# A transformer block on one core: sums moved ahead of the last additions at the MLP's change of layers, and one square root moved into the next QKV

## The chip, the cores and the metric

The kernel runs on one core of one Trainium2 chip. The metric is the device time of one execution in microseconds, as the median of several runs. Beside the runs there is one profiled execution, whose trace is read here. The core has TensorE (PE; its weight loads are listed as PEld), VectorE (DVE), ScalarE (ACT), GpSimd (POOL) and SyncE (SP), which issues most of the transfers. Each engine executes its own queue in order, and semaphores hold an instruction until its inputs and its output's room are ready.

## What is computed

A transformer block with adaptive layer norm on two sequences (rows 0 and 1) of 2048 tokens with 512 features, 16 heads of 32, all in float32:

```python
mod = silu(condition) @ Wada + bada
sh_a, sc_a, gt_a, sh_m, sc_m, gt_m = split(mod, 6)
xm = layernorm(x, g1, be1) * (1 + sc_a) + sh_a
x = x + gt_a * attention(xm, Wqkv, Wproj, bproj)     # causal, softmax
xm = layernorm(x, g2, be2) * (1 + sc_m) + sh_m
h = gelu(xm @ W1 + b1)                               # 512 -> 2048
x = x + gt_m * (h @ W2 + b2)                         # 2048 -> 512
```

## The kernel before

The stages stand one after the other: QKV of row 0, attention of row 0, projection of row 0, QKV, attention and projection of row 1, and then the MLP over both rows. Large products are made by Strassen's scheme in Winograd's form: seven products, named A11, S1, S2, S4, S3, A12, A22 in the order in which `seven` and `two_level` issue them, in place of eight. Their operands are sums and differences of blocks, made by VectorE or GpSimd. The products accumulate in PSUM banks and are combined from there by VectorE (`combine`, line 1728) or copied by ACT.

Most instructions go through `act` or `mm`, which keep them in the order in which the program issues them on their engine. What is queued behind a waiting instruction waits too.

**Projection of a row** (`project_phase`). For each of 16 token tiles: TensorE makes the product, VectorE adds it to the residual (line 1348) and takes the tile's statistics (lines 219 and 222) for the MLP's layer norm, kept in `mv2`. After the last tile `inv_std` turns the 16 variances of the row into `rstd2` and `shift2`: a square root on ACT (line 225), a reciprocal and a product on VectorE (lines 226, 227). They are read only when the MLP normalizes that row's tokens. Right behind the projection of row 0 comes the QKV of row 1: `Qkv.run` issues steps, one outer product each, and after each step calls `tick`, which calls `also(g, n)` with the group g of 512 tokens and the step's number n, from 0. `first` in it (line 1060) lets ACT copy a product's bank, so that the bank can go on.

**The MLP** goes over four groups m of 1024 tokens. For each group the first layer makes the hidden units pair by pair: `pair_of_sets` (m = 1, 2, 3; four pairs p = 0 to 3) makes two units of each half of the 2048 for all tokens, with `two_level` in three phases. Each half of the units (first index) and each half of the tokens (second) gives one of d00, d01, d10, d11, two tiles of 128x512 each. After phase 2 four additions of the third term `t3` finish d11 and d10 (`add`, line 2221), and four gelus (`gelu`, line 2214) follow. In the pairs p = 0 to 2 the additions run on GpSimd and the gelus are put into the next pair's first phase (`later[0]`). In the last pair (`final`) the additions run on VectorE and the gelus follow at once on ACT.

Then `tail` makes the second layer: seven outer sets A11, S1, A12, S2, S3, A22, S4, each of the seven products again (`outer`, one call of `seven`). Each product takes eight matmuls of 256 columns. The operands of the inner products are differences of parts of h (`difference`, line 1631; 128x1024). `Hidden.todo` lists them in the order of use, as keys such as (A11, 2), the second sum of outer set A11. `pop` issues the next one; `need` issues all up to those that a product is about to read. In the last pair's phases four of them are issued through `among`, all to GpSimd: (A11, 1), two parts of T1, (S1, 1). In `tail`, `then(k)` is called after product k of a set and pops one more, to VectorE. The third product (S2) of outer set A11 reads (A11, 2), the fifth (S3) reads (A11, 3), the seventh (A22) reads (A11, 4).

The sums stand in a list of shared tiles (`sums`), PSUM has four banks with the tag "mm" for `outer`, of which each set takes three, and for the transposes of the next group's tokens, which take two after the sets of m < 3.

Of the kernel before, what the change touches and what calls it, by code (L numbers as in the profile page):

```python
# [27 lines left out]
def dit_block_kernel(  # L28
# [192 lines left out]
            act(ins)  # L221
        nc.vector.bn_aggr(mv[:, n, :], st)

    def inv_std(mv, rstd, shift, lo, hi):
        nc.scalar.activation(rstd[:, lo:hi], mv[:, lo:hi, 1], AF.Sqrt, bias=eps)
        nc.vector.reciprocal(rstd[:, lo:hi], rstd[:, lo:hi])
        nc.vector.scalar_tensor_tensor(
            shift[:, lo:hi], mv[:, lo:hi, 0], -1.0, rstd[:, lo:hi], ALU.mult, ALU.mult
        )

    def rows_of(psum, r, b, tag):
# [1066 lines left out]
    def project_phase(row, psum, between):  # L1298

        b = row.b
        with pool(f"proj{b}") as pp:
            n = 0
            ats = list(row.at_s)
            rbs = {1: row.rb_s[1], 2: row.old_queries(), 3: row.rb_s[0]}
            rows_x = [b * NT + i * TQ + t for i in last_order for t in range(TQ)]
            xts = list(row.xt_s)

            def tokens(upto):
                while len(xts) < min(upto, NT):
                    xt = pp.tile([P, D], F32, tag="xt", name="xt", bufs=6)
                    nc.sync.dma_start(xt, x_rows(rows_x[len(xts)]))
                    xts.append(xt)

            row.load_sums(len(units) - 1, len(units))
            tokens(TQ + 6)
            for k, i in enumerate(last_order):
                if k in (0, 1):  # L1320

                    at = pp.tile([P, C, QB], F32, tag="at", name="at", bufs=2)
                    nc.sync.dma_start(at, od[b][last_order[k + 2]])
                    ats.append(at)
                at = ats[k]
                for t in range(TQ):

                    if n == 0:
                        nc.sync.dma_start(rbs[2], wide_d[b][last_order[2]])
                        nc.sync.dma_start(  # L1330
                            rbs[3][:, : C - 1], wide_d[b][last_order[3]][:, : C - 1]
                        )
                    elif n == 3:
                        row.invert(len(units) - 1, len(units))
                    elif n == 4:
                        row.widen(len(units) - 1, rbs[3][:, C - 1, :])

                    tokens(n + 6)
                    nt, xt = rows_x[n], xts[n]
                    if k > 0:  # L1340
                        act(nc.gpsimd.tensor_tensor(xt, xt, bgate, ALU.add))
                    ps = psum.tile([P, D], F32, tag="mm", name="ps_o")
                    for c in range(C):
                        mm(
                            ps, at[:, c, t * P : (t + 1) * P], row.wproj[:, c, :],
                            start=(c == 0), stop=(c == C - 1),
                        )
                    nc.vector.tensor_tensor(xt, ps, xt, ALU.add)
                    stats(pp, xt, nt, mv2, True)
                    nc.sync.dma_start(x1d[nt], xt)  # L1350
                    if k + 1 < NQ:
                        d = ats[k + 1][:, t, :]
                        act(
                            nc.gpsimd.tensor_tensor(d, d, rbs[k + 1][:, t, :], ALU.mult)
                        )
                    between(n)
                    n += 1
        lo, hi = b * NT, (b + 1) * NT
        inv_std(mv2, rstd2, shift2, lo, hi)


    row = Row(0)
# [167 lines left out]
    with pool("qkv1") as qp, pool("ps_qkv1", bufs=6, space=PSUM) as ps_mm:  # L1530
        qkv = Qkv(row, qp, ps_mm)
        qkv.xts[0] = past.next_s

        def between(n):
            if n == 6:
                qkv.load_w(nc.gpsimd)
            if 9 <= n < 12:
                qkv.weight_sum(nc.vector, n - 9)
            elif n == 13:
                qkv.weight_sum(nc.gpsimd, 3)  # L1540
            if n >= 12:
                qkv.token_sum(0, (S1, S2, S3, A22)[n - 12])

            if n < MTT:
                qkv.stats(0, n, True)
            if n in (5, 8):
                qkv.norm(0, n // 8)()
            if n == 8:
                qkv.load_x(1)
            if n >= NT - MTT:  # L1550
                qkv.stats(1, n - (NT - MTT), True)

        project_phase(past, ps_mm, between)

        def also(g, n):
            if (g, n) == (0, 10):
                qkv.value_weight_sums()
            pieces.tick()

        with pool("hl1") as hp:  # L1560
            qkv.load_wv(hp, nc.gpsimd)
            pieces = Pieces()
            spare_q = [row.old_queries().rearrange("p h q -> p (h q)") for _ in range(2)]
            spare_k = [row.key_room(q) for q in (2, 3)]

            def room_1():
                return [
                    (0, blocks_of(value_rows(row, 4, 8), w2p)),
                    (2, blocks_of(value_rows(row, 8, NT), w2p)),
                    (6, blocks_of(spare_q[0], w2p)[:, 1:]),  # L1570
                ]

            def room_3():
                return [
                    (0, blocks_of(value_rows(row, 8, NT), w2p)),
                    (4, blocks_of(spare_k[1], w2p)),
                    (6, blocks_of(spare_q[0], w2p)[:, 1:]),
                ]

            for f, (room, load, start) in enumerate((  # L1580
                (room_2, 0, 6), (room_1, 16, 24), (room_2, 47, 56), (room_3, 74, 80),
            ), FC // 2):
                pieces.plan(f, room, load, start)
            qkv.run(hp, also)
            pieces.done()
# [8 lines left out]
    with ExitStack() as mlp:  # L1594
# [246 lines left out]
        class Hidden:  # L1841
# [3 lines left out]
            def __init__(self):  # L1845
# [6 lines left out]
                ]  # L1852
                self.todo, self.made, self.at = [], set(), 0
                self.slots, self.later, self.flip = {}, {}, False
                self.t = {n: {} for n in OUTER}
                x = {
                    (g, half): {
# [340 lines left out]
            def pair_of_sets(self, p, among):  # L2198
# [13 lines left out]
                def gelu(half, d, j):  # L2212
                    act(
                        nc.scalar.activation(
                            d[j], d[j], AF.Gelu, bias=col(r_b1 + half * HF + fs[j], 1)
                        )
                    )

                def add(engine, d, x):
                    for j in range(2):  # L2220
                        act(engine.tensor_tensor(d[j], d[j], x[j], ALU.add))  # L2221

                def phase(ph, jobs):
# [38 lines left out]
                    4: [lambda: gelu(0, d01, 0)], 6: [lambda: gelu(0, d01, 1)],  # L2262
                }
                phase(2, ((A22, d10, d10), (S3, t3)))
                add(nc.vector if final else nc.gpsimd, d11, t3)
                add(nc.vector if final else nc.gpsimd, d10, t3)
                ends = [
                    lambda d=d, j=j: gelu(1, d, j) for d in (d11, d10) for j in range(2)
                ]
                if final:  # L2270
                    for f in ends:
                        f()
                else:
                    self.later[0] = {r: [f] for r, f in enumerate(ends, 3)}

# [69 lines left out]
        def tail(m, hid, among, each):  # L2345

            u, c22, c11, c12 = Y
            later = []

            def gate(y, half):
                later.extend(lambda i=i: gated(m, y, half, i) for i in range(2))

            for n, dst, base in (
                (A11, u, None),  # L2360
                (S1, c22, None),
                (A12, c11, u),
                (S2, u, u),
                (S3, u, u),
                (A22, u, u),
                (S4, c12, c12),
            ):

                def then(k):
                    if k in (1, 3) and later:  # L2370
                        later.pop(0)()
                    hid.pop()
                    among(n, k)

                hid.outer(n, dst, base, then, each if n == S4 else None)
                if n == A12:
                    gate(c11, 0)
                elif n == S2:
                    combine(c12, u, c22)
                elif n == S3:  # L2380
                    combine(c22, c22, u)
                    gate(c22, 1)
                elif n == A22:
                    gate(u, 1)
                elif n == S4 and not each:
                    gate(c12, 0)
            for f in later:
                f()
# [137 lines left out]
```

## Time and profile before

| | us |
|---|---|
| median of three runs | 2253.81 |
| lowest, highest | 2253.27, 2258.36 |
| profiled execution, its time | 2258.55 |
| profiled execution, its span | 2256.8 |
| mean granted clock of TensorE | 0.995 |

The span goes from the first to the last instruction. A row of waits has the waiting engine, tile and line, what released it, and then total time, number of times and the longest. A row of the timeline has start and duration in us, engine, line, operation, output and inputs, shape and count of merged instructions; in brackets the engine's idle time before it and what ended that. A row of windows has the stretch, its length, the busy time of PE, PEld, DVE, ACT and POOL, the granted clock (1.00 is full), the DMA engines' busy share and GB/s. A row of one line's instructions has their count, duration in ns (min/median/max), first and last start, and shapes. Line numbers are those of the kernel before.

### The profile page before, as it was taken

The page shows a single profiled execution, that of the slowest core. Times are in us where ns is not written, and L with a number is a line of the kernel's source. Part 1 is how long each engine was busy: PE and PEld are TensorE (multiplying, and loading weights), DVE is VectorE, ACT ScalarE, POOL GpSimd, SP SyncE. Part 2 cuts the span into 40 slices and gives each one's busy share as a digit, 9 for nine tenths or more (in the row PEclk, how much of TensorE's full clock was granted, in tenths as well). Part 3 has the DMA queues.
Part 4 walks back from the last instruction along what each step waited for, and adds up shares of the span by engine and source line. Part 5 has one row for each costly group of instructions (what it writes and reads, how often), then busy time and mean ns, then how long its engine had stood idle before and what let it go on. Part 6 is the DMA issues. An engine that isn't in the chain of part 4 may idle for free.

```text
span 2256.8 us, 34324 instructions
## 1 busy us (share of the span) xinstructions
PE 2202.7 (98%) x12273; PEld 1475.6 (65%) x12273; DVE 1577.0 (70%) x3385; ACT 1038.1 (46%) x2132; POOL 1429.7 (63%) x891
## 2 busy tenths in 40 slices
PE   7999999999999999999999999999999999999998
PEld 5887555555543588755555555345788888888887
DVE  4678767777757667777677766664686686677576
ACT  4434555655564243355656556513324423532510
POOL 4253998998983695299989898448417516605520
PEclk9999999999999999999999999999999999999999
DMA  8787142231324799533324123367656455554543
GB/s 271 247 277 192 43 93 70 62 85 48 107 95 147 241 308 312 157 77 74 73 75 95 48 60 133 107 228 262 212 167 213 146 178 180 189 163 159 191 149 108
DMA packets 166627, 340.99 MB, mean 151 GB/s; under 512 B 17216, under 2 KB 49516, under 8 KB 164664
## 3 DMA queue, kind: packets, MB, share of 16 engines
q1 hardware_dynamic: 158080, 302.05, 44.0%
q0 software_dynamic: 8000, 36.21, 4.3%
q8 instruction: 97, 1.59, 0.3%
q14 instruction: 74, 0.61, 0.1%
q10 hardware_dynamic: 376, 0.55, 0.1%
HBM read 246.46 MB, written 100.14 MB: 154 GB/s over the span
## 4 chain that ended last, share of the span: by engine, by line
PE 87%; DVE 6%; POOL 3%; DMA 2%; ACT 1%; issue 1%; SPq 0%; DVEq 0%; ACTq 0%; POOLq 0%
PE ps_a L207 23%; PE st L207 18%; PE ps_b L207 13%; PE o L207 10%; PE s L207 9%; PE ps_c L207 4%; PE sm L207 3%; PE ps_o L207 2%; DVE junk L499 1%; POOL ee L696 1%; PE ps_xt L215 1%; ACT e L671 1%; DVE mx L505 1%; DVE h L2221 1%; PE ps_o L215 1%
## 5 line engine op out<-in xcount | busy, mean ns | idle before, releaser
L671 ACT ACTIVATE e<-st 128x512 f32<-128x512 f32 (+1 forms) x1152 | 574.8, 578 | 362.4 <-PE st L207 313.6
L505 DVE TENSOR_REDUCE mx<-s 128x1 f32<-128x512 f32 x576 | 381.8, 686 | 193.8 <-PE s L207 192.8
L696 POOL TENSOR_TENSOR ee<-ee,e 128x2048 f32<-128x2048 f32 x106 | 485.9, 4584 | 10.3 <-ACT e L671 4.4
L207 PE MATMUL st<-qst,kst 128*128 128x512 f32 (+3 forms) x1280 | 408.6, 386 | 0.0
L207 PE MATMUL s<-kst,qst 128*128 128x512 f32 (+3 forms) x1046 | 380.6, 395 | 5.7 <-DVE mx L505 3.7
L207 PE MATMUL ps_a<-sum,w 128*128 128x256 f32 (+1 forms) x1304 | 340.9, 396 | 12.3 <-DVE sum L1631 11.7
L207 PE MATMUL o<-e,vv 128*32 128x512 f32 (+3 forms) x2560 | 293.2, 537 | 0.3 <-POOL e L683 0.3
L207 PEld LDWEIGHTS st<-qst,kst 128*128 128x128 f32 x1280 | 228.5, 188 | 97.7 <-issue 65.9
L207 PEld LDWEIGHTS ps_a<-sum,w 128*128 128x128 f32 x1304 | 249.2, 193 | 55.3 <-ACT c L2317 12.8
L499 DVE CUSTOM_DVE_ANT_0 junk<-s,causal 128x128 bf16<-128x128 f32 (+3 forms) x470 | 220.7, 470 | 61.0 <-PE s L207 47.0
L207 PEld LDWEIGHTS s<-kst,qst 128*128 128x128 f32 x1046 | 194.8, 188 | 70.7 <-DVE mx L505 17.0
L696 POOL TENSOR_TENSOR ee<-e 128x2048 f32<-128x2048 f32 x42 | 192.5, 4584 | 42.6 <-ACT e L671 42.6
L207 PE MATMUL ps_b<-sum,w 128*128 128x256 f32 (+1 forms) x744 | 186.5, 381 | 0.0
L2221 POOL TENSOR_TENSOR h<-h,h 128x512 f32<-128x512 f32 x96 | 119.3, 1273 | 69.6 <-DVE h L1728 69.6
L207 PEld LDWEIGHTS <-sel 32*128 32x128 bf16 x1152 | 29.5, 91 | 197.0 <-issue 196.1
L207 PEld LDWEIGHTS ps_b<-sum,w 128*128 128x128 f32 x744 | 140.7, 190 | 21.7 <-issue 2.6
L1793 POOL TENSOR_TENSOR sum<-xm 128x256 f32<-128x256 f32 x22 | 23.1, 1052 | 185.4 <-PE ps_a L207 185.4
L505 DVE TENSOR_REDUCE mx<-st 128x1 f32<-128x512 f32 x192 | 131.1, 683 | 0.5
L683 POOL TENSOR_SCALAR_AFFINE_SELECT e<-e 128x512 f32<-128x512 f32 x128 | 83.3, 669 | 67.4 <-ACT e L671 67.3
L207 PEld LDWEIGHTS o<-e,vv 128*32 128x32 f32 x2560 | 59.1, 108 | 92.4 <-issue 73.3
L207 PE MATMUL st<-fold,sel 32*128 32x512 bf16 (+1 forms) x1152 | 117.5, 372 | 1.3
L1067 POOL TENSOR_TENSOR lo<-lo,hi 128x512 fp32r<-128x512 f32 x32 | 40.6, 1275 | 104.4 <-ACT hi L1065 99.4
(264 smaller groups left out, 3549.9 us busy)
## 6 DMA issues: line engine op xcount, KB each, us to landing
w<-w1x SPq DMA_DIRECT2D x42, 896.0 KB
qst<-q SPq DMA_DIRECT2D x128, 256.0 KB
kst<-k SPq DMA_DIRECT2D x128, 256.0 KB
w<-w2d SPq DMA_DIRECT2D x28, 1024.0 KB
w<-w2d SPq DMA_DIRECT2D x28, 768.0 KB
q<-hi SPq DMA_DIRECT2D x32, 256.0 KB
q<-lo SPq DMA_DIRECT2D x32, 256.0 KB
k<-hi SPq DMA_DIRECT2D x32, 256.0 KB
```

What stands on the lines that cost most here:

```text
L207: return tc.keep_in_program_order(nc.tensor.matmul(*args, **kw))
L215: return tc.keep_in_program_order(nc.tensor.transpose(dst, src, ident[:n, :n]))
L499: nc.vector.tensor_tensor_reduce(junk[:, :w], x, causal[:, QB - w :], 1.0, MASKED, ALU.add, ALU.max, m,)
L505: self.vector(nc.vector.tensor_reduce(m, x, axis=AX.X, op=ALU.max))
L671: act(nc.scalar.activation(e4[:, h, :w], sts[h][:, :w], AF.Exp))
L683: nc.gpsimd.affine_select(d, d, pattern=[[0, HC], [1, P]], compare_op=ALU.is_ge, fill=0.0, base=0, channel_multiplier=-1,)
L696: act(nc.gpsimd.tensor_tensor(dst, x, y, ALU.add))
L1067: engine.tensor_tensor(lo, d, hi.bitcast(F32), ALU.subtract)
L1793: act(engine.tensor_tensor(dst, u, v, ALU.subtract))
L2221: act(engine.tensor_tensor(d[j], d[j], x[j], ALU.add))
```

## The change

Row 0's `inv_std` leaves the end of the projection and is issued in the QKV of row 1, in group 0 after step n = 8, with its three instructions kept in program order. Row 1's stays.

In `pair_of_sets` the last additions run on GpSimd in every pair, d10 ahead of d11, and the gelus follow in this order too. In the last pair the sums (A11, 2) to (A11, 4) are issued ahead of the additions, and the four gelus are handed to `tail`, which issues one each after products k = 4, 5, 6 of outer set A11 and after the first product of S1. There `then` pops no sum after products 0 and 1 of A11, so that from k = 2 on each sum has the place it had. At m = 0, which uses `pair`, nothing changes.

```diff
-    def inv_std(mv, rstd, shift, lo, hi):
-        nc.scalar.activation(rstd[:, lo:hi], mv[:, lo:hi, 1], AF.Sqrt, bias=eps)
-        nc.vector.reciprocal(rstd[:, lo:hi], rstd[:, lo:hi])
-        nc.vector.scalar_tensor_tensor(
-            shift[:, lo:hi], mv[:, lo:hi, 0], -1.0, rstd[:, lo:hi], ALU.mult, ALU.mult
+    def inv_std(mv, rstd, shift, lo, hi, keep=False):
+        order = act if keep else (lambda ins: ins)
+        order(nc.scalar.activation(rstd[:, lo:hi], mv[:, lo:hi, 1], AF.Sqrt, bias=eps))
+        order(nc.vector.reciprocal(rstd[:, lo:hi], rstd[:, lo:hi]))
+        order(
+            nc.vector.scalar_tensor_tensor(
+                shift[:, lo:hi], mv[:, lo:hi, 0], -1.0, rstd[:, lo:hi],
+                ALU.mult, ALU.mult,
+            )
         )
...
-        lo, hi = b * NT, (b + 1) * NT
-        inv_std(mv2, rstd2, shift2, lo, hi)
+        if b:
+            inv_std(mv2, rstd2, shift2, NT, 2 * NT)
...
             if (g, n) == (0, 10):
                 qkv.value_weight_sums()
+            elif (g, n) == (0, 8):
+                inv_std(mv2, rstd2, shift2, 0, NT, True)
...
+                self.ends = []
...
                 phase(2, ((A22, d10, d10), (S3, t3)))
-                add(nc.vector if final else nc.gpsimd, d11, t3)
-                add(nc.vector if final else nc.gpsimd, d10, t3)
+                if final:
+                    self.need(*[(A11, n) for n in (2, 3, 4)])
+                add(nc.gpsimd, d10, t3)
+                add(nc.gpsimd, d11, t3)
                 ends = [
-                    lambda d=d, j=j: gelu(1, d, j) for d in (d11, d10) for j in range(2)
+                    lambda d=d, j=j: gelu(1, d, j) for d in (d10, d11) for j in range(2)
                 ]
                 if final:
-                    for f in ends:
-                        f()
+                    self.ends = ends
                 else:
                     self.later[0] = {r: [f] for r, f in enumerate(ends, 3)}
...
                 def then(k):
                     if k in (1, 3) and later:
                         later.pop(0)()
-                    hid.pop()
+                    if hid.ends and (n != A11 or k >= 4):
+                        hid.ends.pop(0)()
+                    if n != A11 or k > 1 or not hid.ends:
+                        hid.pop()
                     among(n, k)
```

## The prediction

> **What bounds the kernel now.** I read the page from the top, then the waits of TensorE alone, then three stretches of the timeline and of the windows. The page:
>
> ```profile
> span 2256.8 us, 34324 instructions
> PE 2202.7 (98%) x12273; PEld 1475.6 (65%) x12273; DVE 1577.0 (70%) x3385; ACT 1038.1 (46%) x2132; POOL 1429.7 (63%) x891
> ...
> PE 87%; DVE 6%; POOL 3%; DMA 2%; ACT 1%; issue 1%; SPq 0%; DVEq 0%; ACTq 0%; POOLq 0%
> ```
>
> TensorE is busy for 98% of the span and holds 87% of the chain that ended last, so only what TensorE waits for, or what slows it, has a price. The waits of TensorE, columns total, times, longest:
>
> ```profile
> PE ps_a L207 <- DVE sum L1631: 11.7, 3, 3.9
> ...
> PE ps_a L207 <- ACT lo L1060: 2.9, 2, 2.7
> ```
>
> The first is the longest total of all of TensorE's waits; its three times are the three changes of layer of the MLP (m = 1, 2, 3). The second holds one wait of 2.7 us, after the first row's projection. The two edits sit on just these places.
>
> **The change of layers.** The timeline at m = 3 (start, duration, engine, line):
>
> ```profile
> 2149.57 0.73 ACT L2214 ACTIVATE h<-h,cols 128x512 f32<-128x512 f32 x1
> ...
> 2150.42 4.70 POOL L1631 TENSOR_TENSOR sum<-h,h 128x1024 f32<-128x1024 f32 x2
> ...
> 2153.17 0.42 DVE L1728 TENSOR_TENSOR h<-h,ps_a 128x256 f32<-128x256 f32 x1
> ...
> 2153.40 1.89 PE L207 MATMUL ps_a<-h,w 128*128 128x256 f32 x8
> 2153.51 6.11 DVE L2221 TENSOR_TENSOR h<-h,y 128x512 f32<-128x512 f32 x4
> ...
> 2155.13 1.89 PE L207 MATMUL ps_b<-sum,w 128*128 128x256 f32 x8
> 2155.20 2.68 POOL L1631 TENSOR_TENSOR sum<-sum,sum 128x1024 f32<-128x1024 f32 x1
> 2155.70 0.72 ACT L2214 ACTIVATE h<-h,cols 128x512 f32<-128x512 f32 x1 [1.10 <-DVE h L2221]
> 2158.46 1.95 ACT L2214 ACTIVATE h<-h,cols 128x512 f32<-128x512 f32 x3 [2.03 <-DVE h L2221]
> 2159.55 1.21 DVE L1631 TENSOR_TENSOR sum<-h,sum 128x1024 f32<-128x1024 f32 x1
> ...
> 2160.68 1.21 DVE L1631 TENSOR_TENSOR sum<-h,h 128x1024 f32<-128x1024 f32 x1
> ...
> 2160.91 3.75 PE L207 MATMUL ps_a<-sum,w 128*128 128x256 f32 x8 [3.89 <-DVE sum L1631]
> ...
> 2167.47 1.89 PE L207 MATMUL ps_a<-sum,w 128*128 128x256 f32 x8
> ```
>
> The outer products of A11 start at 2153.40, one each 1.73 us (2153.40 to 2155.13). The third, S2, needs sum (A11, 2), which is queued on VectorE behind the four last additions (6.11 us): it starts at 2159.55 and TensorE idles 3.89 us. Then TensorE is slow as well: eight matmuls take 3.75 us in place of 1.89, in a window whose granted clock (the column of 0.50) is half:
>
> ```profile
> 2163.00:2164.00 1.00, 1.00 (x3) 0.76 (x3) 1.00 (x2) 0.00 (x0) 0.00 (x0) 0.50 0.00 0
> ```
>
> So the price is read over four products, from S1's start to S3's, which should lie 3 x 1.73 = 5.19 us apart. Here they are 2167.47 - 2155.13 = 12.34 apart: 7.15 lost. The same rows at m = 1 and 2:
>
> ```profile
> 1789.27 1.89 PE L207 MATMUL ps_b<-sum,w 128*128 128x256 f32 x8
> ...
> 1795.04 3.62 PE L207 MATMUL ps_a<-sum,w 128*128 128x256 f32 x8 [3.88 <-DVE sum L1631]
> ...
> 1800.23 1.89 PE L207 MATMUL ps_a<-sum,w 128*128 128x256 f32 x8
> ...
> 1971.74 1.89 PE L207 MATMUL ps_b<-sum,w 128*128 128x256 f32 x8
> ...
> 1977.53 3.75 PE L207 MATMUL ps_a<-sum,w 128*128 128x256 f32 x8 [3.90 <-DVE sum L1631]
> ...
> 1983.62 1.89 PE L207 MATMUL ps_a<-sum,w 128*128 128x256 f32 x8
> ```
>
> 10.96 - 5.19 = 5.77 and 11.88 - 5.19 = 6.69. **Together 19.61 us**, of which 11.67 are the three idle times and 7.94 the slow clock behind them.
>
> *What goes away.* `need` puts sums (A11, 2) to (A11, 4) ahead of the additions. They read d00 after its gelus (ended by 2149.57 + 0.73 = 2150.30) and tiles long free, so (A11, 2) can issue where the first addition does now, at 2153.51.
>
> *What they meet there.* GpSimd has two sums queued that end at 2150.42 + 4.70 = 2155.12. An addition takes VectorE 0.68 us alone and up to 2.83 beside GpSimd; GpSimd takes 1.27:
>
> ```profile
> L2221 POOL TENSOR_TENSOR h<-h,h x96: 1252/1272/1295, 1710.4 to 2149.2; 128x512 f32<-128x512 f32 x96
> ...
> L2221 DVE TENSOR_TENSOR h<-h,y x12: 678/1417/2832, 1787.6 to 2158.9; 128x512 f32<-128x512 f32 x12
> ```
>
> The first addition was issued at 2153.51 and its gelu waited to 2155.70: it ended some 0.55 after GpSimd's sum (2155.12). The next ended near 2158.4, 0.55 after GpSimd's next sum (2155.20 + 2.68 = 2157.88). So the two take turns, one instruction each. VectorE's additions out of PSUM keep 0.42 (2153.17, inside GpSimd's sum), so they take no part. The Trainium skill, "SBUF — State Buffer", section "Who interferes with whom", says that a VectorE instruction with two SBUF inputs and a GpSimd one that reads SBUF lock each other out whole, by issue order; these rows agree.
>
> I play the turns forward (a sum ends 1.21 - 0.13 = 1.08 after its grant, a GpSimd addition 1.10): (A11, 2) ends 2156.2, GpSimd's (S1, 1) 2158.4, (A11, 3) 2159.5, d10's first addition 2160.6, (A11, 4) 2161.7, d10's second 2162.8, a T1 sum 2163.8, d11's first 2164.9, the other T1 sum 2166.0, d11's second 2167.1, (S1, 2) 2168.2. Then GpSimd has nothing left. TensorE, unstalled, asks for (A11, 2) at 2156.86, (A11, 3) at 2160.3, (A11, 4) at 2163.8, and in the next set for (S1, 2) at 2165.5 + 3.45 = 2168.9. **Each is there in time**, by 0.7, 0.8, 2.1 and 0.7 us.
>
> *What is late next.* The combination of the A12 product, behind (S1, 2), ends at 2168.5 in place of 2165.9. It frees one of four PSUM banks; the second product of the next set takes that bank at m = 1 and 2, where the transposes of the next tokens come between (at m = 3 it takes another):
>
> ```profile
> 1805.41 1.04 PE L215 MATMUL ps_xt<-ident,xn 128*128 128x128 f32 x8
> ```
>
> That product is due at 2165.5 + 0.87 + 1.73 = 2168.1 on m = 3's clock, and the bank comes 0.6 us later, with the 0.15 that a release takes (S2 started at 2160.91, its sum ended at 2159.55 + 1.21 = 2160.76). I charge 0.6 twice, **1.2 us**; bounds 0 (the turns go a little faster) and 3 x 2.2 = 6.6 (first rival). VectorE has caught up a set later: in S1 it has seven sums at 1.13 (2159.55 to 2160.68) and three combinations at 0.42, 9.2 us, within 7 x 1.73 = 12.1 us of TensorE.
>
> *The four gelus.* At 0.73 each they go from the end of the pair to the last three steps of A11 (k = 4, 5, 6) and the first of S1. ACT reaches them at 2162.0, 2163.8, 2165.9 and 2168; their inputs are there at 2160.6, 2162.8, 2164.9, 2167.1. Queued behind them are ACT's copies that free banks; none is held, so 0. First reader of the result is (A12, 2), after the last. Without that cover a late addition delays TensorE us for us (slow rival). The swap of d10 and d11 in the other pairs changes which of two equal additions goes first, nothing else: 0.
>
> **The variances of row 0.** The end of its projection:
>
> ```profile
> 771.53 1.03 PE L207 MATMUL ps_a<-xmT,wqk 128*128 128x256 f32 x4
> ...
> 772.40 1.03 PE L207 MATMUL ps_b<-t,wqk 128*128 128x256 f32 x4
> ...
> 773.84 0.69 DVE L1348 TENSOR_TENSOR xt<-ps_o,xt 128x512 f32<-128x512 f32 x1 [3.11 <-POOL xt L1341]
> ...
> 775.30 0.18 DVE L222 BATCH_NORM_AGGREGATE mv<-stat 128x2 f32<-128x6 f32 x1
> 775.52 0.31 ACT L225 ACTIVATE rstd<-mv,eps 128x16 f32<-128x16 f32 x1 [8.35 <-DVE mv L222]
> 775.73 0.36 ACT L1060 ACTIVATE lo<-ps_a 128x256 f32<-128x256 f32 x1
> ...
> 775.86 0.25 DVE L226 RECIPROCAL rstd<-rstd 128x16 f32<-128x16 f32 x1 [0.37 <-ACT rstd L225]
> ...
> 776.14 0.18 DVE L227 SCALAR_TENSOR_TENSOR shift<-mv,rstd 128x16 f32<-128x16 f32 x1
> ...
> 776.15 1.13 PE L207 MATMUL ps_a<-t,wqk 128*128 128x256 f32 x4 [2.73 <-ACT lo L1060]
> ```
>
> ACT stands at the square root until the last token tile's statistics (775.48), with the copies of ps_a and ps_b (products of 771.53 and 772.40) behind it; TensorE needs the first copy and idles **2.73 us**. Moved to the ninth step of the next QKV, the root leaves ACT free: the copies can run as each product ends. VectorE is in the late tile to 775.48, while its first combination is due two products after ps_b's, about 775.1; the six banks of this stage absorb that. At the new place three small instructions cost 0.31 on ACT and 0.25 + 0.18 + 0.37 wait on VectorE, between products 0.87 apart: 0, hidden behind TensorE's next products (the whole 0.7 if VectorE's combination were the next thing asked for). A reload of ACT's table is not to be expected, since the roots here stand among copies as before; the rows of line 225 have three for ten roots, and one more would hold ACT for 1.28, inside what the banks absorb:
>
> ```profile
> L225 ACT ACT_TABLE_LOAD  x3: 1283/1283/1283, 28.4 to 1514.4; - x3
> ```
>
> I take a gain of 2.73; bounds 0 (it is waited for later, below) and 2.73.
>
> **The sum**, against the profiled execution: 2258.55 (span 2256.8) - 19.61 + 1.2 - 2.73 = **2237.4**. That execution lies 4.7 above the median of 2253.81; one unprofiled run was as long (2258.36) and one 2253.27. The three clock dips above are of unequal cost at equal idle times (1.89, 2.79 and 3.26 at 3.9 us), so I read much of the spread as that: it would go with the dips, and all runs come to 2237. If it is something else, 2232.7 follows. I take **2236.5**, nearer the first. The Trainium skill, "TensorE: Matmul & The Clock Gate", section "What's actually happening", has the clock judged over free-running windows of about 3.4 us, so the same idle time would cost differently from run to run; the unequal dips fit that. No run here shows it yet.
>
> **Rivals.**
> *GpSimd first* (0.08): the turn at 2155.12 goes to (S1, 1), and (A11, 2) ends at 2157.88 + 1.08 = 2158.96: TensorE idles 2.2 us at each change, 6.6 in all, with a dip for each at up to 7.94 in all: 2243 to 2251. For it: GpSimd's next sum is issued 0.08 after the last. Against: VectorE got that turn in the rows above.
> *Row 0's gain is given back* (0.08): GpSimd's work of the next QKV starts with weight loads that do not move, and TensorE, 2.7 us ahead, waits for it: 2239. Against it, GpSimd runs dry before it is next on the path:
>
> ```profile
> 861.79 1.27 POOL L1067 TENSOR_TENSOR lo<-lo,hi 128x512 fp32r<-128x512 f32 x1 [10.78 <-ACT hi L1065]
> ```
>
> *The change does not do what it says* (0.04): something else holds (A11, 2), and only row 0 gains: 2258.55 - 2.73 = 2255.8, less the spread some 2252. Against: every input named above is early.
> *Slower: ACT held behind a late gelu* (0.04). If VectorE's sums are granted in a row and GpSimd only after (S1, 4), near 2170.8, d10's second addition ends at 2173.3; behind its gelu on ACT is A22's copy, and the bank that this frees is due at 2167.2. TensorE waits to 2174.6, 7.4 us, and with a dip of 7.94 / 3 = 2.65 loses 10.0 at each change: 30.1 against 22.3 gained, 2266. It decides where that addition ends past about 2169; I have 2162.8.
>
> **How the numbers follow.** The forecast, all parts as summed, has 0.76, with its own range of 2231 to 2242. The range for 8 in 10 goes a little into the first rival: 2230 to 2244. What a measurement can tell from no change is about 0.3%, 6.8 us: below 2247.05 is faster. Forecast, row 0's return and most of the first rival: 0.90. Same: the rest of that rival and the change without effect, 0.06. Slower: 0.04.
>
> **What would show it.** TensorE's wait for L1631 gone from its list, and S1 to S3 5.2 us apart at each change; granted clock 1.00 there; L2221's VectorE group empty, its GpSimd group twelve longer; the L1631 sums after 2153 stretched to 2.2 or 3 us by turns; the ACT wait for L222 shorter and the 2.73 us gap gone. Wrong it would be if a wait of TensorE for PSUM banks (ACT copies or VectorE combinations) of over 2 us stands at the head of outer set S1, or if a gelu's wait for GpSimd is long on ACT.

## The result and the profile after

| | before | after |
|---|---|---|
| median of seven runs each, us | 2257.31 | 2248.74 |
| lowest, highest, us | 2253.27, 2260.64 | 2247.25, 2251.03 |
| profiled execution: span, us | 2256.8 | 2245.5 |
| granted clock of it | 0.995 | 0.997 |

The ratio of the times is 0.9969, with a 95% interval of 0.9959 to 0.9979: faster, by 0.3%, some 7 us (the two medians stand 8.6 apart). The forecast was 2236.5 us, 17 us less than the median of three runs known then, in a range of 2230 to 2244. The direction held, the size did not. The page of the kernel after:

```profile
span 2245.5 us, 34306 instructions
...
PE 86%; DVE 6%; POOL 3%; DMA 2%; ACT 1%; issue 1%; SPq 0%; ACTq 0%; DVEq 0%; POOLq 0%
```

The page looks as before. The difference is in TensorE's waits (engine, tile and line, releaser: total, times, longest). Lines have moved by up to seven: the sums' L1631 is now L1637, the combinations' L1728 is L1734, the additions' L2221 is L2228, and the gelus' L2214 is L2221.

```profile
PE ps_a L207 <- DVE y L1734: 7.7, 3, 2.6
```

The 11.7 us for L1631 are gone from the list, as forecast. In their place stand three waits of 2.6 us, again one at each change of layers, but for a combination and not for a sum. Timeline at m = 3, over the seven products of outer set A11, with what VectorE and GpSimd do beside them:

```profile
2144.98 1.89 PE L207 MATMUL ps_a<-h,w 128*128 128x256 f32 x8
2145.09 2.69 DVE L1637 TENSOR_TENSOR sum<-h,sum 128x1024 f32<-128x1024 f32 x1
...
2146.78 3.22 POOL L1637 TENSOR_TENSOR sum<-sum,sum 128x1024 f32<-128x1024 f32 x1
...
2147.70 3.38 DVE L1637 TENSOR_TENSOR sum<-h,h 128x1024 f32<-128x1024 f32 x1
...
2149.96 8.87 POOL L2228 TENSOR_TENSOR h<-h,y 128x512 f32<-128x512 f32 x4
...
2151.00 2.28 DVE L1637 TENSOR_TENSOR sum<-h,sum 128x1024 f32<-128x1024 f32 x1
...
2153.21 2.29 DVE L1637 TENSOR_TENSOR sum<-h,h 128x1024 f32<-128x1024 f32 x1
2153.62 1.89 PE L207 MATMUL ps_c<-h,w 128*128 128x256 f32 x8
...
2155.42 0.41 DVE L1734 TENSOR_TENSOR y<-c,ps_b 128x256 f32<-128x256 f32 x1
...
2155.75 1.95 DVE L1637 TENSOR_TENSOR sum<-h,h 128x1024 f32<-128x1024 f32 x1
...
2157.62 0.41 DVE L1734 TENSOR_TENSOR y<-c,ps_a 128x256 f32<-128x256 f32 x1
...
2158.09 5.14 PE L207 MATMUL ps_a<-sum,w 128*128 128x256 f32 x16 [2.58 <-DVE y L1734]
```

Read VectorE's rows from the top: sums (A11, 2), (A11, 3), (A11, 4), the first T1 sum (2153.21), the combination of S4's product out of ps_b, the second T1 sum (2155.75), and then the combination of S3's product out of ps_a (2157.62), ended at 2158.03. The seventh product, A22, accumulates onto what S3 left in ps_a, so it may not start before S3's combination has read the bank (in `seven`, `last` reads bank a after S3, and A22 goes on in the same bank). A22 is due 1.73 after A12, at 2153.62 + 1.73 = 2155.35, some 10.4 after A11's start. It starts at 2158.09, and TensorE idles 2.58 us. The row at that start merges sixteen matmuls, A22's eight and those of the next set's first product; they take 5.14 us in place of 2 x 1.73 + 0.16 = 3.62. The window of the first microsecond has the granted clock (the column after the five engines) at half:

```profile
2158.00:2159.00 1.00, 0.92 (x2) 0.83 (x3) 1.00 (x2) 0.00 (x0) 0.82 (x1) 0.50 0.00 0
```

At m = 1 the whole price can be read off two starts. From A11 to the transposes behind its set lie seven products, 7 x 1.73 = 12.1 us at full pace. Before, those starts were 1787.54 (1.73 ahead of S1's 1789.27) and 1805.41: 17.9, 5.8 lost. After:

```profile
1782.89 1.89 PE L207 MATMUL ps_a<-h,w 128*128 128x256 f32 x8
...
1791.53 1.89 PE L207 MATMUL ps_c<-h,w 128*128 128x256 f32 x8
1796.00 3.55 PE L207 MATMUL ps_a<-sum,w 128*128 128x256 f32 x8 [2.58 <-DVE y L1734]
1799.38 1.04 PE L215 MATMUL ps_xt<-ident,xn 128*128 128x128 f32 x8
```

16.5, so 4.4 lost. TensorE's matmuls are the same in number (12273) and order in all traces, so two spans can be split by comparing the start of the same matmul. Of the 11.3 us between these two spans the three changes of layers gave 6.7, the stage from the end of row 0's projection to the first change gave 2.5, and the first 30 us, which the change does not touch, 1.9; the remaining 0.2 lie between those stretches.

### The profile page after: what moved, and what is told of

Same layout as the page of the kernel before. It is cut to its first block, busy times and chain, and to the rows that moved or that the text cites. A ratio compares the mean times of both kernels' runs of the same rounds, so it can differ in the third digit from the quotient of the medians.

```text
span 2245.5 us, 34306 instructions
## 1 busy us (share of the span) xinstructions
PE 2197.9 (98%) x12273; PEld 1473.3 (66%) x12273; DVE 1578.2 (70%) x3373; ACT 1038.3 (46%) x2132; POOL 1456.7 (65%) x903
## 4 chain that ended last, share of the span: by engine, by line
PE 86%; DVE 6%; POOL 3%; DMA 2%; ACT 1%; issue 1%; SPq 0%; ACTq 0%; DVEq 0%; POOLq 0%
PE ps_a L207 22%; PE st L207 19%; PE ps_b L207 13%; PE o L207 10%; PE s L207 9%; PE ps_o L207 4%; PE ps_c L207 3%; PE sm L207 3%; DVE sum L1637 2%; DVE junk L503 1%; POOL ee L700 1%; PE ps_xt L215 1%; ACT e L675 1%; DVE mx L509 1%; PE ps_o L215 1%
## 5 line engine op out<-in xcount | busy, mean ns | idle before, releaser
L2228 POOL TENSOR_TENSOR h<-h,h 128x512 f32<-128x512 f32 x96 | 119.3, 1271 | 69.8 <-DVE h L1734 69.8
```

## The experiments

No experiment leaves anything out of the computation. The first seven differ from the changed kernel as their diffs show, and the eighth is the kernel before. Ratios are against the kernel before, run on the same chip. The first four shared one chip, the last four another; the kernel before had a median of 2254.69 on the first and 2257.45 on the second.

**1. The root alone.** The MLP's part is put back as it was.

```diff
-                if final:
-                    self.need(*[(A11, n) for n in (2, 3, 4)])
-                add(nc.gpsimd, d10, t3)
-                add(nc.gpsimd, d11, t3)
+                add(nc.vector if final else nc.gpsimd, d11, t3)
+                add(nc.vector if final else nc.gpsimd, d10, t3)
...
                 if final:
-                    self.ends = ends
+                    for f in ends:
+                        f()
```

> Only the square root of row 0 is moved; the MLP is as before. My theory, from the two traces (TensorE's idle time of 2.73 us after row 0's projection is gone, and the stages behind it start 2.2 to 2.5 us earlier): 2.0 to 2.7 us shorter than the kernel before, ratio 0.9988 to 0.9992; the three MLP waits of 3.9 us are there unchanged. Rival, that what the root gains is given back at GpSimd's work of the next QKV: 0 to 0.7 us.

Measured: 2255.10, ratio 0.9994 (0.9985 to 1.0004), a gain of 1.4 us that may be anything from a loss of 0.9 to a gain of 3.4. The waits of 11.7 us are back. The root's move alone cannot be told from no change, and neither the theory nor its rival is decided.

**2. The MLP's part alone.** The root stays at the end of row 0's projection.

```diff
-        if b:
-            inv_std(mv2, rstd2, shift2, NT, 2 * NT)
+        lo, hi = b * NT, (b + 1) * NT
+        inv_std(mv2, rstd2, shift2, lo, hi)
...
-            elif (g, n) == (0, 8):
-                inv_std(mv2, rstd2, shift2, 0, NT, True)
```

> Only the MLP part of the change; the root of row 0 stands where it was. Theory: the 2.73 us idle time after row 0's projection is back, and the MLP gives 6 to 7 us (each change of layers loses 4.3 us in place of 5.8 to 7.2): ratio 0.9969 to 0.9976. Rival, that the two parts do not add (the root's place shifts the MLP's clock windows): more than 8 us or less than 5.

Measured: 2251.11, ratio 0.9976 (0.9966 to 0.9986), with the three waits for a combination at 2.6 us as in the changed kernel. 0.9994 x 0.9976 = 0.9970, the ratio of both together, so the parts add within their intervals. Most of what is missing is missing in the MLP. The expected return of 2.73 us did not come: the wait that the root's move was to remove is a third of what it was in the first profile, with the root in its old place:

```profile
774.31 1.13 PE L207 MATMUL ps_a<-t,wqk 128*128 128x256 f32 x4 [0.92 <-ACT lo L1064]
```

**3. The T1 sums behind the combination.** `then` pops none after products 2 and 3 of A11 either, so the two T1 sums come behind S3's combination. The turns of VectorE and GpSimd stay.

```diff
-                    if n != A11 or k > 1 or not hid.ends:
+                    if n != A11 or k > 3 or m == 0:
                         hid.pop()
```

> The changed kernel, but outer set A11 pops no sum after products 2 and 3 either, so that both T1 sums are issued behind the combination of product S3. Theory (the A22 product accumulates into bank a, which the combination of S3 must have read, and that stands on VectorE behind the T1 sums): TensorE's wait for L1734 of 2.58 us goes at all three changes, the clock stays 1.00, and the MLP gets the rest of what I forecast, some 13 us: 2235 to 2238, ratio to before 0.990 to 0.992. Rival A (GpSimd's additions and their turns hold the sums that TensorE multiplies): nothing changes, 2246 to 2250. Rival B (the wait moves on to sum (S1, 2) in the next set, now two steps later): a new wait of TensorE for L1637 of 1 to 3 us, 2240 to 2247.

Measured: 2241.07, ratio 0.9930 (0.9916 to 0.9944), outside the 2235 to 2238 that were expected. The three waits for L1734 are gone, as the theory had it, and the granted clock is 0.999; but the waits for sums that rival B named came as well. Two pops fewer leave VectorE two sums behind, which shows some 70 us later, in TensorE's waits and its timeline:

```profile
PE ps_a L207 <- DVE sum L1637: 2.9, 3, 1.1
```

```profile
1851.48 1.99 PE L207 MATMUL ps_a<-sum,w 128*128 128x256 f32 x8 [1.14 <-DVE sum L1637]
```

**4. d11's additions issued later on GpSimd**, at the product k = 6, so that the turns might end sooner.

```diff
                 add(nc.gpsimd, d10, t3)
-                add(nc.gpsimd, d11, t3)
+                if not final:
+                    add(nc.gpsimd, d11, t3)
...
+                    late = ends[2]
+                    ends[2] = lambda: (add(nc.gpsimd, d11, t3), late())
                     self.ends = ends
```

> The changed kernel, but in the last pair d11's two additions are issued after the last product of A11 in place of right behind d10's, so that two of GpSimd's four turns are out of the way of VectorE's sums ahead of A22. Theory (order on VectorE, two T1 sums ahead of the combination): VectorE reaches the combination of S3 0.65 us earlier and no more, the wait for L1734 falls from 2.58 to about 1.9 us, time 2245 to 2248. Rival A (the turns are the cause): the wait falls by two turns of 1.1 us to 0.4 us or less, and the clock stays up: 2238 to 2242.

Measured: 2247.29, ratio 0.9963 (0.9948 to 0.9977). The time lies in the range that was expected, but the wait is unchanged, where 1.9 us were expected. The timeline at m = 3 says why this told nothing apart:

```profile
2149.84 8.87 POOL L2228 TENSOR_TENSOR h<-h,y 128x512 f32<-128x512 f32 x4
```

The four additions run at the same place and pace as in the changed kernel (8.87 us from 2149.96). GpSimd has its own queue, and nothing stood in it between d10's and d11's additions; being issued later among TensorE's products holds nothing back there. The expectation overlooked that. The next experiment takes the turns away in another manner.

**5. The additions on VectorE, each just ahead of its gelus.** GpSimd has none, so there are no turns; the T1 sums stand where the changed kernel has them, ahead of S3's combination.

```diff
-                add(nc.gpsimd, d10, t3)
-                add(nc.gpsimd, d11, t3)
+                else:
+                    add(nc.gpsimd, d10, t3)
+                    add(nc.gpsimd, d11, t3)
...
-                    self.ends = ends
+                    self.ends = [
+                        lambda: (add(nc.vector, d10, t3), ends[0]()), ends[1],
+                        lambda: (add(nc.vector, d11, t3), ends[2]()), ends[3],
+                    ]
```

> The changed kernel, but in the last pair the four additions go to VectorE, d10's after product S3 of A11 (k = 4), d11's after its last product (k = 6), each pair of them ahead of its first gelu. GpSimd then has nothing left to take turns with after (S1, 1), and the T1 sums keep their places ahead of the combination of S3. Theory (it is the turns that make VectorE late; the two T1 sums alone, at 1.13 us each, would let it reach that combination 10.3 us after A11's start, and A22 is due at 10.4): the wait for L1734 falls from 2.58 to 0.3 us or less, the clock stays 1.00, 2235 to 2240, ratio 0.990 to 0.993. Rival (the order alone does it: two sums ahead of the combination cost A22 its time on any engine's load): a wait of 1.5 us or more stays, 2243 to 2249.

Measured: 2238.52, ratio 0.9918 (0.9904 to 0.9933). The wait is gone, as expected. Timeline at m = 1:

```profile
1784.42 1.89 PE L207 MATMUL ps_a<-h,w 128*128 128x256 f32 x8
...
1791.57 1.21 DVE L1637 TENSOR_TENSOR sum<-h,h 128x1024 f32<-128x1024 f32 x1
...
1792.71 0.41 DVE L1734 TENSOR_TENSOR y<-c,ps_b 128x256 f32<-128x256 f32 x1
...
1793.04 1.21 DVE L1637 TENSOR_TENSOR sum<-h,h 128x1024 f32<-128x1024 f32 x1
...
1794.17 0.41 DVE L1734 TENSOR_TENSOR y<-c,ps_a 128x256 f32<-128x256 f32 x1
1794.51 1.28 DVE L2228 TENSOR_TENSOR h<-h,y 128x512 f32<-128x512 f32 x2
1794.78 1.89 PE L207 MATMUL ps_a<-sum,w 128*128 128x256 f32 x8
```

The same two T1 sums stand ahead of S3's combination, but take 1.21 us each instead of 2.29 and 1.95, since GpSimd is out of the way. The combination ends at 1794.58, 10.2 after A11's start, and A22 starts on time at +10.4. The first addition follows it.

**6. Experiment 3 with the two pops made up.** The sums left out come after products 5 and 6 of A11, behind S3's combination.

```diff
-                    if n != A11 or k > 1 or not hid.ends:
+                    if n != A11 or k > 3 or m == 0:
+                        hid.pop()
+                    if n == A11 and k > 4 and m:
                         hid.pop()
```

> As e3, the T1 sums behind the combination of S3, but after products 5 and 6 of A11 two sums are issued each, so that from the next set on the list of sums stands where it stood. Theory (e3's new waits of 1.14, 1.14 and 0.6 us come from sums that were two steps late in every later set): they go, 2.9 us shorter than e3, 2233 to 2239, ratio 0.9895 to 0.9925. Rival (they come from tiles of the sums that come free later): the waits for L1637 stay near 2.9 us in all and the time is e3's.

Measured: 2237.64, ratio 0.9912 (0.9897 to 0.9927); the waits of experiment 3 for sums are gone too. The additions are still GpSimd's here. Timeline at m = 1:

```profile
1786.16 1.89 PE L207 MATMUL ps_a<-h,w 128*128 128x256 f32 x8
...
1794.99 0.42 DVE L1734 TENSOR_TENSOR y<-c,ps_a 128x256 f32<-128x256 f32 x1 [0.22 <-PE ps_a L207]
1795.33 1.33 DVE L1637 TENSOR_TENSOR sum<-h,h 128x1024 f32<-128x1024 f32 x1
...
1796.52 1.89 PE L207 MATMUL ps_a<-sum,w 128*128 128x256 f32 x8
```

Now VectorE waits 0.22 us for S3's product instead of coming late to it, the T1 sum follows, and A22 is on time. Compared matmul by matmul with the first profile of the kernel before, the three changes of layers gave 5.8, 6.7 and 7.2 us here: the whole 19.6 that the prediction had priced. No wait of TensorE for a bank stands at the head of the next set, for which 1.2 had been charged.

**7. The additions on VectorE right behind the sums**: late work in front of S3's combination, without GpSimd.

```diff
-                add(nc.gpsimd, d10, t3)
-                add(nc.gpsimd, d11, t3)
+                add(nc.vector if final else nc.gpsimd, d10, t3)
+                add(nc.vector if final else nc.gpsimd, d11, t3)
```

> The changed kernel with the four last additions on VectorE, in their place right behind the three sums; gelus and all else as changed. No turns, but 4 x 0.61 us of additions more on VectorE ahead of the combination of S3. Theory (TensorE waits for what stands on VectorE ahead of that combination, turns or instructions alike): VectorE reaches it 12.7 us after A11's start in place of 13.0, the wait is 2.2 to 2.4 us at each change, 2244 to 2249. Rival (the engines' turns alone matter): the wait is under 0.5 us, 2235 to 2240.

Measured: 2250.45, ratio 0.9964 (0.9953 to 0.9976). Timeline at m = 1, where A22 was due at 1803.85 + 1.73 = 1805.58:

```profile
1795.22 1.89 PE L207 MATMUL ps_a<-h,w 128*128 128x256 f32 x8
...
1802.36 2.49 DVE L2228 TENSOR_TENSOR h<-h,y 128x512 f32<-128x512 f32 x4
...
1803.85 1.89 PE L207 MATMUL ps_c<-h,w 128*128 128x256 f32 x8
...
1807.37 0.41 DVE L1734 TENSOR_TENSOR y<-c,ps_a 128x256 f32<-128x256 f32 x1
1807.84 3.68 PE L207 MATMUL ps_a<-sum,w 128*128 128x256 f32 x8 [2.10 <-DVE y L1734]
```

The four additions cost 2.49 us of VectorE's time and no turns, and the combination comes to +12.2 all the same. The wait is 2.10 us where 2.2 to 2.4 were expected, and the median 1.5 us above the expected range. (The profiled execution, with a span of 2257.0, is the slowest of the seven: it also has waits of 1.99 and 2.91 us in the QKV after row 0, of which more below.)

**8. The kernel before once more**, one profile, for what differs from execution to execution.

> The kernel before, for another profile. Theory (the idle time after row 0's projection, 2.73 us in the first profile and 0.92 in e2's, which has the root in the same place, hangs on when the last tile's x lands): it differs from 2.73 again, between 0.5 and 3 us, and the three waits of the MLP are 3.9 us each with slow clock behind them of 1.5 to 3.5 us each. Rival (0.92 in e2 came from the change of the MLP): 2.6 to 2.9.

Measured: 2254.69, one run, span 2253.0; TensorE's waits for L1631 are 11.7 us as in the first profile. But the first of them brought no slow clock, where 1.5 to 3.5 us had been expected behind each. Timeline at m = 1 and the window behind the wait:

```profile
1792.98 1.97 PE L207 MATMUL ps_a<-sum,w 128*128 128x256 f32 x8 [3.89 <-DVE sum L1631]
1794.79 1.89 PE L207 MATMUL ps_b<-h,w 128*128 128x256 f32 x8
```

```profile
1794.00:1795.00 1.00, 1.00 (x6) 0.87 (x5) 1.00 (x1) 0.01 (x1) 0.00 (x0) 1.00 0.00 0
```

In the first profile the same eight matmuls behind 3.88 idle took 3.62 us. And the wait at row 0 is smaller here, with what GpSimd waited for ahead of it:

```profile
770.21 1.27 POOL L1341 TENSOR_TENSOR xt<-xt,bgate 128x512 f32<-128x512 f32 x1 [1.25 <-DMA xt<-in_x_dram]
...
773.90 1.13 PE L207 MATMUL ps_a<-t,wqk 128*128 128x256 f32 x4 [0.67 <-ACT lo L1060]
```

The same kernel, 0.67 us instead of 2.73.

## Why the prediction was wrong

**The step that failed** is "What is late next". "Each is there in time" held for the four sums that it names, but it took A22 to be free to start when (A11, 4) is there. For what comes after the sums the prediction looked only at the bank that A12's combination frees. It did not ask what A22 needs apart from (A11, 4): the reading of its own bank, ps_a, by S3's combination, which stands on VectorE behind both T1 sums. That wait was put at nothing, without a reason. The numbers for it were all there. The turns as played put the second T1 sum at +12.6 and so S3's combination, 0.42 longer, at +13.0; A22 was due at +10.4. That is 2.6 to 2.7 us of idle time; measured were a combination ended at +13.05 and 2.58 us at m = 3, and 2.57 to 2.58 at each of the three changes. With the slow clock behind it the three losses are 13.0 us (4.4 + 4.3 + 4.3), where 1.2 had been charged, for another bank. The sum would have come to 2237.4 - 1.2 + 13.0 = 2249.2; the profiled execution had 2247.25, with 1.9 us of the difference won in the first 30 us, and the median is 2248.74. The prediction's sign of being wrong, a wait of TensorE of over 2 us for a combination's bank at the head of set S1, came one product earlier than it had looked for it.

That it is this and no other wait, experiments 3, 5, 6 and 7 show from both sides. The turns alone do no harm (6: turns, but the T1 sums behind the combination). The T1 sums alone do none (5: both ahead of it, at 1.21 us each). Other work in front of the combination harms in the same way (7). What decides is when VectorE reaches S3's combination, which takes 0.41 us: at +8.8 in 6, +9.8 in 5, +12.2 in 7 and +12.6 in the changed kernel, against a product due at +10.4.

**What held.** The turns came about as played: (A11, 2) ended at +2.8 (forecast +2.8), (A11, 3) at +6.1 (+6.1), (A11, 4) at +8.3 (+8.3), the T1 sums at +10.5 and +12.7 (+10.4 and +12.6), all from A11's start at 2144.98. The sums were in time for their products and the wait for them went. So the first rival, GpSimd first, did not come to be. That VectorE's sums take 2.28 beside GpSimd's additions and 1.21 without them, and the additions 8.87 / 4 = 2.22 beside the sums and 1.27 alone, while combinations out of PSUM keep 0.41, agrees with what the Trainium skill states ("SBUF — State Buffer", "Who interferes with whom"): two SBUF inputs on VectorE and a reading GpSimd lock each other out, and a combination out of PSUM, with one SBUF input, takes no part. The late gelus cost nothing; the slower rival did not occur. ACT does wait for the additions:

```profile
2152.24 0.72 ACT L2221 ACTIVATE h<-h,cols 128x512 f32<-128x512 f32 x1 [1.50 <-POOL h L2228]
```

but no wait of TensorE for ACT stands there.

**Row 0: the mechanism was right, the term was mis-sized.** 2.73 us was one execution's value; with the root in its old place the wait was 0.67 in experiment 8 and 0.92 in experiment 2. It goes with the landing of the last tile of x, since GpSimd's work on that tile waits for the load: 1.25 us in experiment 8, 1.39 in experiment 2, and 3.48 in the first profile:

```profile
772.55 1.26 POOL L1341 TENSOR_TENSOR xt<-xt,bgate 128x512 f32<-128x512 f32 x1 [3.48 <-DMA xt<-in_x_dram]
```

After the move there is no gap at that place, and the root stands later, among the next QKV's products:

```profile
770.23 1.03 PE L207 MATMUL ps_b<-t,wqk 128*128 128x256 f32 x4
771.10 1.03 PE L207 MATMUL ps_a<-t,wqk 128*128 128x256 f32 x4
...
778.36 0.30 ACT L226 ACTIVATE rstd<-mv,eps 128x16 f32<-128x16 f32 x1
```

Just behind that place all seven profiles with the root moved have gained 2.9 us on the first profile. Within 60 us part of the gain is gone again, as the second rival had it, though it is VectorE that TensorE waits for there and not GpSimd's work behind the weight loads. TensorE's waits between 765 and 835 us with the root's move alone:

```profile
PE ps_a L207 <- DVE lo L1083: 0.8, 1, 0.8
PE ps_a L207 <- DVE vv L1139: 0.6, 1, 0.6
```

Whether these two waits come from the move or from the same late loads was not settled; the first also stands with the root in its old place, at 0.4 us in experiments 2 and 8. Over the whole stage up to the first change of layers six of the seven gained 1.1 to 3.4 us on it (experiment 7 lost 7.6), but the two further profiles with the root in its old place gained 0.2 and 1.9 as well. The timed gain is 1.4 us with an interval that holds zero.

The new place was priced at 0, or 0.7 us at most, and that does not hold in every execution. The last of the root's three instructions took 0.17 to 0.18 us on VectorE in its old place and 0.17 to 1.21 in six of the profiles at the new one. In the profile of experiment 7 it took 4.28 and held the combinations behind it, for which TensorE waited 1.99 us and then ran slow:

```profile
781.77 4.28 DVE L229 SCALAR_TENSOR_TENSOR shift<-mv,rstd 128x16 f32<-128x16 f32 x1
...
782.30 1.28 POOL L1258 TENSOR_TENSOR kst<-kst,qst 128x512 f32<-128x512 f32 x1
783.52 1.28 POOL L1258 TENSOR_TENSOR qst<-kst 128x512 f32<-128x512 f32 x1
...
784.75 1.26 POOL L1258 TENSOR_TENSOR kst<-kst 128x512 f32<-128x512 f32 x1
...
786.77 3.23 PE L207 MATMUL ps_a<-t,wqk 128*128 128x256 f32 x8 [1.99 <-DVE lo L1083]
```

It ended as the third of these GpSimd instructions did, at 786.0. By 790 us that execution had lost 3.9 us again, more than the 2.9 gained. Its later wait of 2.91 us stands behind a transfer that landed late; whether it follows from the first is not shown.

**The spread.** The prediction put 2236.5 under its sum because it read the few us between executions as the clock's dips, which would go. In part that is so: dips differ, as experiment 8 shows, and kernel 6, which has none at the changes, spreads over 2.1 us in its four runs (2235.72 to 2237.83). But 3 and 5, which have none either, still spread over 5.3 and 4.5 us. Two other sources appear in the profiles. The first 30 us, with the same work (their last three columns are granted clock, DMA share and GB/s), of before and then of after:

```profile
0.00:30.00 30.00, 18.37 (x65) 9.56 (x65) 16.62 (x45) 10.90 (x18) 16.34 (x32) 0.94 0.85 282
```

```profile
0.00:30.00 30.00, 18.13 (x72) 10.53 (x73) 16.87 (x47) 12.50 (x21) 16.78 (x33) 1.00 0.88 293
```

The after trace is 1.9 us ahead there, with a higher clock and more moved. Of the ten profiles four had the clock of 1.00 in that stretch and came out of it 1.3 to 2.2 us ahead of the first; six had 0.94 and lay within 0.6 of it. Kernels with the change stand in both groups, so 1.9 of the 11.3 us between the two spans are not its doing. The other source is the waits after row 0's projection, 0 to 2.9 us. What makes up the rest stays open.

**Without the failed step** the forecast would have been near: experiment 6 keeps both edits and takes the T1 sums out of the way, and comes to 0.9912 x 2257.31 = 2237.4 us. It and experiment 5 beat both kernels of this case; their intervals overlap, so neither is shown to be the better.

## What to carry to other kernels

When work is put in front on an in-order engine, list everything that stands behind it on that engine up to the next idle time, and set each against its own due time, not only the operands that were in question: here the sums had 0.7 us to spare and the next bank reader, behind two fillers, was 2.6 late. A product that accumulates into a bank that was read in between waits for that reader as it does for an operand. And filler that is not due (the T1 sums, which no product of that set reads) goes behind the reader of a bank, all the more while a second engine doubles its length.

## What the hardware showed unexpectedly

An idle time of TensorE does not fix what the slow clock behind it costs. Behind 3.88 to 3.89 us at m = 1 the same eight matmuls took 3.62 us in one execution and 1.97, at the full clock, in another. Eight matmuls of the same shape took 3.55 behind the shorter 2.58 us and 3.68 behind 2.10 in experiment 7, while behind 1.14 in experiment 3 they took 1.99. The Trainium skill ("TensorE: Matmul & The Clock Gate", "What's actually happening") has windows of about 3.4 us that run free of the program, which fits a price that changes at equal idle time; its advice to keep gaps under about 3 us ("Why this matters for your kernels") does not save this kernel, in which eight matmuls took nearly twice their time behind 2.1 us already.

Between an engine that would take 1.21 us for a sum and one that would take 1.27 for an addition, neither ran through at the changes of layers: they alternated one by one at 2.2 us each, as long as both had work. In the QKV of experiment 7 they did not: one VectorE instruction that takes 0.17 us alone ended only as the third GpSimd instruction in a row did, 4.28 us after its start. What decides between the two cases is not shown.
